# Eight late tiles' second FFN placed between the last scores and the last values; the second stack load three slots earlier

## The chip, the core and the metric

The kernel runs on one core of a Trainium2 chip. The core has five engines that each work through their own instructions in order: PE (TensorE, matrix products), DVE (VectorE), ACT (ScalarE), POOL (GpSimd) and SP (SyncE, which here issues nearly all DMA transfers). They meet only at semaphores. The metric is the device time of one execution in microseconds; a number given for a kernel is the median of several runs. Smaller is better.

## The reference

The input x has 4 batches of 4096 rows of 512 numbers. Three blocks follow each other, each with a residual:

```python
x = x + 0.5 * ffn(layernorm(x), weight, bias)
x = x + attn(layernorm(x), qkv_w, qkv_b, rpb, proj_w, proj_b)
x = x + 0.5 * ffn(layernorm(x), weight, bias)
```

`ffn` is one 512 x 512 product whose two operands are first quantised, in blocks of 32 along the row, to a 6-bit floating-point grid with a scale for each block. `attn` is neighbourhood attention with 16 heads of 32: row i attends to the 13 rows around it (shifted inwards at both ends of a batch), with a relative bias `rpb`:

```python
attn = einsum('bhld,bhlkd->bhlk', q * SCALE, k[:, :, nbr, :]) + rpb[:, bidx]
out  = einsum('bhlk,bhlkd->bhld', softmax(attn), v[:, :, nbr, :])
x_attn = out.reshape(B, L, C) @ proj_w.T + proj_b
```

The two FFNs use the same weights.

## The kernel before

**Tiles and items.** The 16384 rows are 128 tiles of 128 rows (numbered t = 0 to 127). Four tiles make a group of 512 rows; there are 32 groups (8 for each batch). Attention works in items m = 0 to 127: item m is one group and one quarter of the heads (four heads, 128 columns). A product in full precision is split into high and low halves in f16, so each is 12 matmuls of 128 x 512 (function `product`, line 151): low x high, high x low and high x high over four chunks of the inner dimension.

**The order.** The work is put in order by hand. Every stage is a generator; `begin(slot, stage, rank)` enters it at a slot, and each `yield n, rank` moves the rest n slots on. The slots are run one after the other, lower ranks first within a slot, and what a slot emits is appended to the engines' queues in just that order. One step is STEP = 7 slots and handles one tile and one item. The offsets of line 561 place the stages: first FFN of tile t at 7t+5, V product at 7t+20, for item m the query and key projections at 7m+38 (`project_qk`), scores and softmax at 7m+42 (`softmax`), values' products at 7m+59 (`attend`), the output projection of tile t at 7t+93 (`project_out`) and its second FFN 12 slots later (F2 = 12, `second_half`). For the last tiles `out_slot` and `second_slot` give other slots, since the last group's output can only be projected when item 127 has its values.

**A second FFN.** After the output projection of tile t in slot s, `quantised_norms` for the slot s+2 runs over eight slots: POOL forms the factors of the layer norm, ACT applies them, DVE takes the block maxima, POOL scales, ACT rounds to 8 bits, POOL scales back, ACT casts the high half (`hlq`), and in slot s+9 DVE forms the low half and SP issues the transpose `xT<-hlq` (line 205). `second_half(t)` is then 12 matmuls on PE (`pmf<-wt,xT`), in the next slot a multiply-and-add into x on DVE (line 275) and the store of x to the output on SP (line 555). Up to tile 112 the norm of the third block shares its operations with the first norm of tile t+15; from tile 113 on it stands alone.

**The softmax of an item.** Scores on PE in slot a = 7m+42 (144 small matmuls, line 433); then a+1 bias sums on DVE, a+2 maximum on DVE, a+3 subtraction on POOL (467), a+4 exponential on ACT (469), a+5 sums on DVE (472), a+6 scaling on POOL (476), a+8 casts on ACT (480, 481), a+10 the low half on POOL (483) and the transpose `pT<-p` on SP (485). The values' products (line 503, 72 small matmuls) follow in slot a+17, then the copies of their result into `ring` by ACT (530) and DVE (536).

**Values from memory.** The V product is stored to DRAM (line 312), and for each group two "stacks" are loaded back with `load_stack` (line 409), one for each half of the heads, three or six transfers each: the first in slot k+46, the second in slot k+56, with k = 28 x group; rank 9 puts them last in their slot. The second is read by the values of slots k+73 and k+80. There are two buffers (`vsp`), and the one that the second load takes was last read in slot k+52.

**Buffers that matter.** `xp`: 20 buffers of 128 x 512 f32, for the residual tiles x (loaded in slot 7t-18, freed with the store after the second FFN), and for some temporaries of tiles from 123 on. `xtp`: 3 buffers for the transposed xT. `hlp`: 1 buffer for hlq (tiles from 123 on take one of `xp`). `ps_m`: 3 PSUM buffers shared by all 12-matmul products.

The lines that set the late slots:

```python
if i in (-4, -3):                                   # i = t - LAST, LAST = 123
    return (n_items - 1) * STEP + PV + i            # tiles 119, 120: slots 944, 945
if i in (-2, -1):
    return out_slot(NT - 1) + 3 + i                 # tiles 121, 122: slots 960, 961
return out_slot(t) + F2                             # 113 to 118: slots 896, 903, ... 931
```

The last scores stand in slot 931, the values of item 126 in 941, those of item 127 in 948; the output products of tiles 120, 121 and 122 in 929, 933 and 937, those of 123 to 127 in 951 to 959.

Of the kernel before, what the change touches and what calls it, by code (L numbers as in the profile page):

```python
# [26 lines left out]
F32 = mybir.dt.float32  # L27
F16 = mybir.dt.float16
# [9 lines left out]
P = 128  # L38
# [26 lines left out]
def macaron_kernel(  # L65
# [13 lines left out]
    n_batch, length, dim = x.shape  # L79
    xf = x.rearrange("b l c -> (b l) c")  # L80
    of = out.rearrange("b l c -> (b l) c")
    KC = dim // P
# [3 lines left out]
    NT = n_batch * length // P  # L86
# [6 lines left out]
    ps_m = ctx.enter_context(tc.tile_pool(name="ps_m", bufs=3, space=PSUM))  # L93
    ps_s = ctx.enter_context(tc.tile_pool(name="ps_s", bufs=1, space=PSUM))
    ps_v = ctx.enter_context(tc.tile_pool(name="ps_v", bufs=1, space=PSUM))
    xp = ctx.enter_context(tc.tile_pool(name="xp", bufs=20))
    yp = ctx.enter_context(tc.tile_pool(name="yp", bufs=1))
    sm = ctx.enter_context(tc.tile_pool(name="sm", bufs=2))
    q8p = ctx.enter_context(tc.tile_pool(name="q8p", bufs=1))
# [1 line left out]
    xtp = ctx.enter_context(tc.tile_pool(name="xtp", bufs=3))  # L101
# [27 lines left out]
    def bc(t, n):  # L129

        return t.unsqueeze(2).to_broadcast([t.shape[0], t.shape[1], n])
# [30 lines left out]
    def begin(slot, stage, rank=5):  # L162
        slots.setdefault(slot, []).append((rank, stage))
# [19 lines left out]
    def factors(t, which, mv, n=1):  # L183

        rs = sm.tile([P, n], F32, tag=f"rs{which}{n}", name=f"rs{which}_{t}")
        nc.gpsimd.tensor_scalar(  # L186
            rs, mv[:, :n, 1], XS ** -2, LN_EPS * XS ** -2, ALU.mult, ALU.add
        )
        nc.gpsimd.tensor_tensor(rs, rs, minus_half[:, :n], ALU.pow)
        nb = sm.tile([P, n], F32, tag=f"nb{which}{n}", name=f"nb{which}_{t}")  # L190
        if n == 1:
            nc.gpsimd.tensor_scalar(nb, mv[:, 0, 0:1], rs, -1.0, ALU.mult, ALU.mult)  # L192
        else:
            nc.gpsimd.tensor_tensor(nb, mv[:, :n, 0], rs, ALU.mult)
            nc.gpsimd.tensor_scalar(nb, nb, -1.0, None, ALU.mult)
        return rs, nb

    def high(y, hl):

        nc.scalar.copy(hl[:, :, 0, :], y)  # L200

    def low(y, hl, dst):

        nc.vector.tensor_tensor(hl[:, :, 1, :], y, hl[:, :, 0, :], ALU.subtract)  # L204
        nc.sync.dma_start_transpose(out=dst, in_=hl.rearrange("p u s k -> p (u s k)"))
# [14 lines left out]
    def quantised_norms(slot):  # L220

        tiles, mv = together.pop(slot)
        n = len(tiles)
        rs, nb = factors(slot, "q", mv[0], n)
        yield 1, 1

        spare = tiles[0][0] >= NT - GROUP - 1
        if spare:
            y = xp.tile([P, dim], F32, tag="x", name=f"yq{slot}").unsqueeze(1)
        else:  # L230
            y = yp.tile([P, 2, dim], F32, tag="yq", bufs=2, name=f"yq{slot}")[:, :n]
        for u, (t, _) in enumerate(tiles):
            nc.scalar.activation(  # L233
                y[:, u], xs[t], AF.Identity, bias=nb[:, u : u + 1], scale=rs[:, u : u + 1]
            )
        yield 1, 1
        yb = y.rearrange("p u (n q) -> p (u n) q", q=QB)
        sc = sm.tile([P, 2 * NB], F32, tag="sc", bufs=4, name=f"sc{slot}")[:, : n * NB]
        nc.vector.tensor_reduce(sc, yb, AX.X, ALU.max, apply_absolute_value=True)
        nc.vector.scalar_tensor_tensor(  # L240
            sc, sc, F8_SCALE / Q_MAX, least[:, : n * NB], ALU.mult, ALU.max
        )
        r = sm.tile([P, 2 * NB], F32, tag="r", bufs=4, name=f"r{slot}")[:, : n * NB]
        nc.vector.reciprocal(r, sc)  # L244
        yield 1, 1
        nc.gpsimd.tensor_tensor(yb, yb, bc(r, QB), ALU.mult)  # L246
        yield 1, 1
        q8 = q8p.tile([P, 2, dim], F8, tag="q8", name=f"q8_{slot}")[:, :n]
        nc.scalar.activation(q8, y, AF.Identity, bias=nudge, saturate=False)  # L249
        yield 1, 3  # L250
        nc.gpsimd.tensor_tensor(  # L251
            yb, q8.rearrange("p u (n q) -> p (u n) q", q=QB), bc(sc, QB), ALU.mult
        )
        yield 1, 3
        if spare:
            hl = xp.tile([P, dim], F32, tag="x", name=f"hlq{slot}").bitcast(F16)
            hl = hl.rearrange("p (u s k) -> p u s k", u=1, s=2)
        else:
            hl = hlp.tile([P, 2, 2, dim], F16, tag="hlq", name=f"hlq{slot}")[:, :n]
        high(y, hl)  # L260
        yield 1, 1
        xT = xtp.tile([P, 2, 2, KC, P], F16, tag="xT", name=f"xT{slot}")
        low(y, hl, xT[:, :n].rearrange("p u s c q -> p (u s c) q"))
        for u, (t, _) in enumerate(tiles):
            ys[t] = xT[:, u]
# [75 lines left out]
    n_items = n_batch * NG * KC  # L341
# [199 lines left out]
    def project_out(t, slot):  # L541

        r = t * P % RING
        pm = ps_m.tile([P, dim], F32, tag="mm", name=f"pmo_{t}")
        product(
            pm, lambda s, c: ring[:, s, c, r : r + P], lambda s, c: wt[:, s, c, PO : PO + dim]
        )
        yield 1, 8
        nc.vector.scalar_tensor_tensor(xs[t], pm, cp, xs[t], ALU.mult, ALU.add)
        moments(slot, t, "n3")  # L550

    def second_half(t):

        yield from ffn(t, "f2")
        nc.sync.dma_start(out=of[t * P : (t + 1) * P, :], in_=xs.pop(t))
# [3 lines left out]
    STEP = 7  # L559

    F1, V, QK, SC, PV, OUT, F2 = 5, 2 * STEP + 6, 5 * STEP + 3, 6 * STEP, 8 * STEP + 3, 13 * STEP + 2, 12
# [4 lines left out]
    def one(f, *args):  # L566
        f(*args)
        return
        yield

    LAST = NT - GROUP - 1

    def out_slot(t):


        i = t - LAST
        if i >= 0:
            return (n_items - 1) * STEP + PV + 3 + 2 * i
        if i >= 1 - GROUP:
            return LAST * STEP + PV + 21 + 4 * i  # L580
        return t * STEP + OUT

    def second_slot(t):

        i = t - LAST
        if i in (-4, -3):
            return (n_items - 1) * STEP + PV + i
        if i in (-2, -1):
            return out_slot(NT - 1) + 3 + i
        return out_slot(t) + F2  # L590

    for t in range(NT):
        k = t * STEP
        begin(k - 18, one(load, t), 0)
        enlist(k - 10, t, "n1")
        if not 0 < t < EARLY:
            begin(k - 11, one(moments, k - 10, t, "n1"), 1)
        begin(k + F1, first_half(t))
        begin(k + V, values(t))
        begin(k + F1, one(add_bias, t, half_ffn_b), 8)  # L600
        at = out_slot(t)
        begin(at - 5, one(add_bias, t, after_b), 8)
        enlist(at + 2, t, "n3")
        begin(at, project_out(t, at + 2))
        begin(at + 6 if t < LAST else second_slot(t) - 2, one(add_bias, t, half_ffn_b), 8)
        begin(second_slot(t), second_half(t))
    for slot in together:
        if slot >= EARLY * STEP - 10:
            begin(slot, quantised_norms(slot), 1)
    for m in range(n_items):  # L610
        k = m * STEP
# [3 lines left out]
    for n in range(n_batch * NG):  # L615
        k = n * GROUP * STEP
        b, g = divmod(n, NG)
        begin(k + 6 * STEP + 4, one(load_stack, b, g, 0), 9)
        begin(k + 8 * STEP, one(load_stack, b, g, 1), 9)


    with tc.tile_pool(name="setup", bufs=1) as sp, tc.tile_pool(name="scratch", bufs=2) as scr:
# [18 lines left out]
        for _ in quantised_norms(-10):  # L641
            pass
        chunks = (8, 9, 10, 11, 12, 13, 14, 15, 0, 4, 1, 5, 2, 6, 3, 7)
        for o in chunks:
            w, i = (qkv_w, o) if o < 3 * KC else (proj_w, o - 3 * KC)
# [87 lines left out]
        def large(name, o, dt=F32):  # L733
            return scr.tile(
                [P, NB, QB], dt, tag=name, bufs=3 if name == "wu_" else KC, name=f"{name}{o}"
            )

        for o in range(KC):
# [7 lines left out]
            for i, b in enumerate((w_hi, w_lo)):  # L746
                u = large("wu_", f"{o}_{i}")
# [17 lines left out]
        for t in range(1, EARLY):  # L765
            moments(t * STEP - 10, t, "n1")
            for _ in quantised_norms(t * STEP - 10):
                pass
# [94 lines left out]
        slot = first  # L863
# [48 lines left out]
```

## Time and profile before

| | |
|---|---|
| time, median of 3 runs (lowest to highest) | 2408.76 us (2407.12 to 2414.85) |
| the profiled execution: whole time | 2401.24 us |
| its span, first to last instruction | 2399.4 us |
| granted TensorE clock, mean | 0.993 |
| PE busy | 2278.8 us, 95% of the span |
| DVE busy | 2015.3 us, 84% |
| POOL busy | 1989.0 us, 83% |
| ACT busy | 1327.1 us, 55% |
| DMA | 360.58 MB, mean 150 GB/s |

How to read the lines that follow in the text: times are microseconds from the start of the span. In a line of the order of one engine come start, duration, engine, line of the kernel, operation, output<-inputs by name, shape of one instruction and how many were merged (x12). A bracket at the end is the time in which the engine was idle before, and what ended it; "issue" means that the profile shows nothing that it waited for. The page's row of tenths cuts the span in 40 slices of 60 us; 9 means busy for 90% or more. In the chain that ended last each step is followed back to what released it, so its shares say which engine the time hangs on. Matmuls overlap: the time from one product's start to the next one's is what it costs PE.

### The profile page before, as it was taken

How to read it: one execution, taken by the hardware profiler on the slowest of the kernel's cores; microseconds unless marked ns; L12 is line 12 of the kernel's file. 1: busy time of each engine (PE TensorE's matmuls, PEld its weight loads, DVE VectorE, ACT ScalarE, POOL GpSimd, SP SyncE). 2: the span in 40 equal slices, each digit the busy share in tenths (PEclk: the TensorE clock that was granted, in tenths of full speed). 3: DMA queues.
4: the chain of work that ended last, by engine and by line, in shares of the span. 5: the costliest groups of instructions: out<-in, count | busy, mean ns of one | idle time of the engine just before them, and what ended most of it. 6: DMA issues, size and time to landing. Idle time of an engine off the chain costs nothing.

```text
span 2399.4 us, 82333 instructions
## 1 busy us (share of the span) xinstructions
PE 2278.8 (95%) x35539; PEld 1114.0 (46%) x35539; DVE 2015.3 (84%) x3588; ACT 1327.1 (55%) x2080; POOL 1989.0 (83%) x2012
## 2 busy tenths in 40 slices
PE   0799999999999999999999999999999999999987
PEld 0244444444444444444444444444444444444442
DVE  8789888888888888888888888888888888888775
ACT  4455555555555556555555555555555555555442
POOL 5578888888888888888888888888888888888677
PEclk9899999999999999999999999999999999999998
DMA  5788888787787877778867778777778887777753
GB/s 153 145 150 153 158 164 158 148 157 151 145 161 156 152 150 159 146 153 162 161 145 156 150 146 167 153 154 147 159 139 156 158 158 146 162 148 143 137 115 90
DMA packets 925700, 360.58 MB, mean 150 GB/s; under 512 B 718876, under 2 KB 889752, under 8 KB 925336
## 3 DMA queue, kind: packets, MB, share of 16 engines
q1 hardware_dynamic: 924992, 354.79, 75.6%
q8 instruction: 278, 4.55, 0.8%
q10 hardware_dynamic: 344, 0.53, 0.1%
q14 instruction: 86, 0.70, 0.1%
HBM read 110.15 MB, written 67.29 MB: 74 GB/s over the span
## 4 chain that ended last, share of the span: by engine, by line
PE 89%; DVE 4%; DMA 3%; issue 1%; POOL 1%; ACT 1%; SPq 0%; DVEq 0%; ACTq 0%; POOLq 0%
PE pmqk L151 27%; PE pmf L151 26%; PE pmo L151 14%; PE pmv L151 13%; PE ps L433 6%; PE pv L503 3%; DMA xT<-hlq 2%; DVE hlq L204 0%; DVE fw L749 0%; DMA x<-hln 0%; DVE qk L373 0%; DVE stn L180 0%; POOL x L564 0%; ACT ring L530 0%; DVE whl L779 0%
## 5 line engine op out<-in xcount | busy, mean ns | idle before, releaser
L151 PE MATMUL pmf<-wt,xT 128*128 128x512 f16 x3048 | 703.1, 381 | 17.8 <-DMA xT<-hlq 17.7
L151 PE MATMUL pmqk<-x,wt 128*128 128x512 f16 x3072 | 707.7, 380 | 6.2 <-DMA x<-hln 5.4
L151 PEld LDWEIGHTS <-xT 128*128 128x128 f16 x3048 | 297.0, 98 | 386.1 <-DMA xT<-hlq 29.3
L151 PEld LDWEIGHTS <-wt 128*128 128x128 f16 x3072 | 290.0, 98 | 343.1 <-issue 9.7
L151 PE MATMUL pmv<-wt,x 128*128 128x512 f16 x1536 | 353.8, 380 | 5.1 <-DMA x<-hln 5.1
L151 PE MATMUL pmo<-wt,ring 128*128 128x512 f16 x1536 | 355.3, 381 | 2.6 <-issue 2.6
L246 POOL TENSOR_TENSOR yq<-yq,r 128x1024 f32<-128x1024 f32 (+1 forms) x141 | 246.2, 1746 | 130.8 <-DVE r L244 130.8
L564 POOL TENSOR_TENSOR x<-x,half_ffn_b 128x512 f32<-128x512 f32 x256 | 327.4, 1279 | 0.1
L275 DVE SCALAR_TENSOR_TENSOR x<-pmf,coef,x 128x512 f32<-128x512 f32 x256 | 179.5, 701 | 165.2 <-PE pmf L151 164.7
L530 ACT ACTIVATE ring<-pv 128x510 f16<-128x510 f32 (+8 forms) x224 | 82.3, 414 | 400.5 <-PE pv L503 400.5
L310 ACT CAST vt<-pmv 128x512 f16<-128x512 f32 x128 | 74.9, 585 | 389.3 <-PE pmv L151 389.3
L180 DVE BATCH_NORM_STATS2 stn<-x 128x6 f32<-128x512 f32 x384 | 265.3, 691 | 8.9 <-DMA x<-in_L_attn_x_dram 0.2
L251 POOL TENSOR_TENSOR yq<-q,sc 128x1024 f32<-128x1024 fp8e4 (+1 forms) x141 | 246.7, 1749 | 0.4 <-ACT q L249 0.4
L151 PEld LDWEIGHTS <-x 128*128 128x128 f16 x1536 | 150.5, 98 | 187.6 <-DMA x<-hln 5.6
L373 DVE SCALAR_TENSOR_TENSOR qk<-pmqk,qk_b,qk 128x512 f16<-128x512 f32 x256 | 190.6, 744 | 53.8 <-ACT qk L369 53.0
L476 POOL TENSOR_TENSOR sf<-sf,total 128x714 f32<-128x714 f32 (+2 forms) x128 | 178.6, 1395 | 44.2 <-DVE total L474 25.0
L151 PEld LDWEIGHTS <-ring 128*128 128x128 f16 x1536 | 140.2, 98 | 161.5 <-issue 4.2
L186 POOL TENSOR_SCALAR rsq<-mv 128x2 f32<-128x2 f32 (+1 forms) x141 | 131.3, 931 | 96.0 <-DVE mv L181 93.8
L249 ACT ACTIVATE q<-yq,nudge 128x1024 fp8e4<-128x1024 f32 (+1 forms) x141 | 149.9, 1063 | 108.0 <-POOL yq L246 99.8
L369 ACT ACTIVATE qk<-pmqk,qk_b 128x512 f16<-128x512 f32 x256 | 176.1, 688 | 53.2 <-PE pmqk L151 52.1
L233 ACT ACTIVATE yq<-x,nbq,rsq 128x512 f32<-128x512 f32 x254 | 193.0, 804 | 20.8 <-POOL nbq L192 20.2
L467 POOL TENSOR_TENSOR sf<-sf,top 128x714 f32<-128x714 f32 (+2 forms) x128 | 180.4, 1409 | 20.0 <-DVE top L465 19.8
(145 smaller groups left out, 3466.9 us busy)
## 6 DMA issues: line engine op xcount, KB each, us to landing
vs<-vd SPq DMA_DIRECT2D x144, 357.0 KB
x<-in_L_attn_x_dram SPq DMA_DIRECT2D x128, 256.0 KB
vd<-vt SPq DMA_DIRECT2D x128, 256.0 KB
out_dram<-x SPq DMA_DIRECT2D x128, 256.0 KB
vs<-vd SPq DMA_DIRECT2D x24, 378.0 KB
vs<-vd SPq DMA_DIRECT2D x24, 315.0 KB
rows<-in_L_attn_qkv_w_dram SPq DMA_DIRECT2D x12, 256.0 KB
xT<-hlq SPq DMA_TRANSPOSE x141
```

Of the source, the lines that this page charges most:

```text
L151: nc.tensor.matmul(pm, lhs(a, c), rhs(b, c), start=(n == 0), stop=(n == 3 * KC - 1))
L180: nc.vector.bn_stats(st, xs[t])
L233: nc.scalar.activation(y[:, u], xs[t], AF.Identity, bias=nb[:, u : u + 1], scale=rs[:, u : u + 1])
L246: nc.gpsimd.tensor_tensor(yb, yb, bc(r, QB), ALU.mult)
L249: nc.scalar.activation(q8, y, AF.Identity, bias=nudge, saturate=False)
L251: nc.gpsimd.tensor_tensor(yb, q8.rearrange("p u (n q) -> p (u n) q", q=QB), bc(sc, QB), ALU.mult)
L275: nc.vector.scalar_tensor_tensor(xs[t], pm, cf, xs[t], ALU.mult, ALU.add)
L369: nc.scalar.activation(t[:, s, 0, KN:], pms[s], AF.Identity, bias=bias)
L373: nc.vector.scalar_tensor_tensor(t[:, s, 1, KN:], pms[s], bias, t[:, s, 0, KN:], ALU.add, ALU.subtract)
L467: nc.gpsimd.tensor_tensor(s, s, bc(top[:, :n], KN), ALU.subtract)
L476: nc.gpsimd.tensor_tensor(s, s, bc(total[:, :n], KN), ALU.mult)
L564: nc.gpsimd.tensor_tensor(xs[t], xs[t], b, ALU.add)
```

## The change

The second FFN of the eight tiles 113 to 120 (`HELD`) is moved. Those of 113 to 118, which stood at slots 896, 903, 910, 917, 924 and 931, now stand at 932, 935, 938, 942, 943 and 944; those of 119 and 120 move from 944 and 945 to 945 and 946. All eight are now between the last scores (931) and the last values (948). Their DVE sums and stores move with them. Their norms and the transposes into xT stay where they were; since these xT are kept longer, each takes a buffer of `xp` instead of one of the three of `xtp`, and `xp` has 23 buffers instead of 20. Apart from that, in every group the load of the second stack is issued in slot k+53 instead of k+56.

```diff
-    xp = ctx.enter_context(tc.tile_pool(name="xp", bufs=20))
+    xp = ctx.enter_context(tc.tile_pool(name="xp", bufs=23))
...
-        xT = xtp.tile([P, 2, 2, KC, P], F16, tag="xT", name=f"xT{slot}")
+        if tiles[0][0] in HELD and tiles[0][1] == "n3":
+            xT = xp.tile([P, dim], F32, tag="x", name=f"xT{slot}").bitcast(F16)
+            xT = xT.rearrange("p (u s c q) -> p u s c q", u=1, s=2, c=KC)
+        else:
+            xT = xtp.tile([P, 2, 2, KC, P], F16, tag="xT", name=f"xT{slot}")
...
+    HELD = range(NT - 15, NT - 7)
...
-        if i in (-4, -3):
-            return (n_items - 1) * STEP + PV + i
+        if t in HELD:
+            return (n_items - 1) * STEP + PV - (16, 13, 10, 6, 5, 4, 3, 2)[t - HELD[0]]
...
-        begin(k + 8 * STEP, one(load_stack, b, g, 1), 9)
+        begin(k + 7 * STEP + 4, one(load_stack, b, g, 1), 9)
```

## The prediction

> **What bounds the kernel now.** I read the page first (rows of tenths, then the chain that ended last), then the order of PE's instructions over the last 200 us with the idle time in front of each, then all of PE's gaps, then SP's order, then the other engines over the end.
>
> ```profile
> PE   0799999999999999999999999999999999999987
> PE 89%; DVE 4%; DMA 3%; issue 1%; POOL 1%; ACT 1%; SPq 0%; DVEq 0%; ACTq 0%; POOLq 0%
> ```
>
> PE sets the time: it is full from the third slice to the last two and carries 89% of the chain. Between 170 and 2230 us it is busy for 2043.84 of 2060.00 us at a clock of 1.00. After 2330 us it works 47.26 of 69.40 us, at a mean clock of 0.89. So work taken off PE's full stretch and put into the holes of the end is time won. The holes, in PE's order (start, duration, instruction, count, and in brackets the idle time before it with what ended it):
>
> ```profile
> 2324.55 2.75 PE L151 MATMUL pmf<-wt,xT 128*128 128x512 f16 x12
> 2327.23 1.35 PE L433 MATMUL ps<-qk 32*32 32x84 f16 x144
> 2328.51 2.76 PE L151 MATMUL pmo<-wt,ring 128*128 128x512 f16 x12
> 2331.21 0.72 PE L503 MATMUL pv<-pT,vs 126*32 126x30 f16 x72
> 2331.86 2.76 PE L151 MATMUL pmo<-wt,ring 128*128 128x512 f16 x12
> 2341.80 0.83 PE L503 MATMUL pv<-pT,vs 126*32 126x30 f16 x72 [7.18 <-DMA pT<-p]
> 2342.74 7.25 PE L151 MATMUL pmf<-wt,xT 128*128 128x512 f16 x24
> 2355.65 0.76 PE L503 MATMUL pv<-pT,vs 126*32 126x30 f16 x72 [5.66 <-DMA pT<-p]
> 2356.33 15.14 PE L151 MATMUL pmo<-wt,ring 128*128 128x512 f16 x60
> ```
>
> Line 2 is the last scores (item 127); the two L503 lines with brackets are the values of items 126 and 127. Both wait for their transposed probabilities: 7.18 + 5.66 = 12.84 us of idle PE. Between them lie the second FFNs of tiles 119 and 120 (x24); line 1 is that of tile 118.
>
> **Part 1, the held FFNs.** Tiles 113 to 118 leave slots 896 to 931 (PE starts at 2248.84, 2264.90, 2279.91, 2292.49, 2306.79, 2324.55) and go to 932, 935, 938, 942, 943, 944; 119 and 120 move one slot. The same instructions run. A product of 12 takes 2.59 to 2.69 us from start to start.
>
> *What the full stretch gives.* Tile 113: 2.68 us. Tile 114: its scores stand at 2267.59; without its FFN and the 0.90 us that this waits for its xT they can follow the V product at 2263.93: 3.66. Tile 115: 2.68. Tiles 116 and 117 give almost nothing: with no V product left, the FFN is all that stands between the key projection and the scores, which need the low half of the keys. DVE ends that (L373) at 2294.63 and 2308.97, 0.6 and 0.5 us before the scores now start (2295.19, 2309.48). Those scores moreover stop inside for 1.50 and 2.41 us on "issue", until 7.3 and 8.1 us after a stack load began; if the load is what ends these, even that is lost. I take 0 (ends: 0, and 4.7 if the stops vanish too). Tile 118: the output product of tile 120 stands there, so its 2.68 us go, but only for what follows it. Sum ahead of tile 120's product: 2.68 + 3.66 + 2.68 = 9.0.
>
> *What the end can take.* The two waits are ends of a chain with no PE product on it after tile 120's: its sum (DVE L549 at 2325.62), POOL from 2327.31 almost without a break to 2335.5 (L483 of item 126), pT's DMA landing at 2341.7; then for item 127:
>
> ```profile
> 2342.77 0.62 ACT L200 CAST hlq<-yq 128x512 f16<-128x512 f32 x1 [3.30 <-DMA xT<-hlq]
> 2345.81 0.19 POOL L186 TENSOR_SCALAR rsq<-mv 128x1 f32<-128x1 f32 x1 [2.54 <-DVE mv L181]
> 2349.19 1.56 POOL L483 TENSOR_TENSOR p<-sf,p 128x756 f16<-128x756 f32 x1
> ```
>
> The single hlq buffer makes ACT wait for the preceding transpose, DVE's sum and moments of tile 122 queue behind that, POOL's factors behind those, and L483 and pT behind these. This chain moves by the 9.0, no more: values 126 become possible at 2332.7, 127 at 2346.6. PE now has, from the scores at 2315.5: 1.35 scores, FFN 113, product 121, values 125, FFN 114, product 122, FFN 115, that is 5 x 2.6 + 0.7, to 2330.6; a wait of 2.1; values 126; FFNs 116 to 118, to 2341.4. FFN 119 needs a third PSUM buffer back, that of 116, which DVE (slot 943, behind the low half of tile 121 and the ring) frees 0.75 us after its 2351.97, shifted 2343.7: a wait of 2.3. FFN 120 ends at 2348.9, so values 127 come 2.3 us after they could. That is covered: tile 123's product stops for the ring's low half (DVE L536, ended at 2360.06), which queues behind the low half of tile 122 (2357.42 to 2358.6, held by a DMA and not by PE). One more FFN sum (0.7) now lies there; the ring is ready at 2351.8 instead of 2360.06. **The end comes 8.3 us sooner.** Without the cover it would be 2.3 less.
>
> *Other queues.* SP gets a 256 KB store of tiles 113 to 115 ahead of the transposes of items 126 and 127; each waits for a DVE sum that is done 1 us or more before SP reaches the transpose. A store's bytes in front of pT: 0 to 1 us, taken as 0. Buffers: 15 x tiles and 8 held xT make 23 at most, so the pool holds them; three more buffers free no load elsewhere, since a load at slot 7t-18 finds buffers free since slot 7t-34.
>
> *A rule against the row.* The Trainium skill ("TensorE: Matmul & The Clock Gate", HAM oscillation) says that an idle gap over about 3.4 us puts the array on half clock, some 3.4 us of work long. The trace agrees: pmo matmuls last 609 to 634 ns until 2359.5, then 379. By the rule both holes cost 1.7 us more, and filling them brings 12.84 + 3.4 = 16.2. By the rows it is 8.3: the cold FFNs lie inside the wait for pT, the cold products inside the wait for the ring. The remaining waits of 2.1 and 2.3 are below the rule's gap. I go by the rows.
>
> **Part 2, the second stack load.** Same three transfers, from slot k+56 to k+53: on SP it passes one store of V (L312), which waits for DVE, and lands right behind the transposes of slot k+53, exactly where the first stack's load already stands, a step earlier.
>
> ```profile
> 1373.19 1.66 SPq L409 DMA_DIRECT2D vs<-vd  x3
> ...
> 1383.40 2.72 SPq L485 DMA_TRANSPOSE pT<-p  x1
> 1386.44 3.00 SPq L205 DMA_TRANSPOSE xT<-hlq  x1
> ...
> 1396.02 1.67 SPq L409 DMA_DIRECT2D vs<-vd  x3
> ...
> 1401.42 6.32 SPq L485 DMA_TRANSPOSE pT<-p  x1
> 1407.84 3.05 SPq L205 DMA_TRANSPOSE xT<-hlq  x1
> ```
>
> After the first stack SP spends 2.72 us on pT; after the second 6.32, and xT goes out late. PE then waits for xT:
>
> ```profile
> 1413.05 2.76 PE L151 MATMUL pmf<-wt,xT 128*128 128x512 f16 x12 [1.59 <-DMA xT<-hlq]
> 1740.19 1.02 PE L151 MATMUL pmo<-wt,ring 128*128 128x512 f16 x4 [2.13 <-issue]
> ```
>
> Nine such xT gaps stand between 170 and 2270 us, every one 14 to 17 us after a second stack's load and none after a first's: 7.05 us. Less the 0.90 counted above, **6.15 go**. What is late next is pT, used a step later. At the start the second stack of group 0 (142.26) makes PE wait 4.11 us for x2; SP stood idle 1.7 before the V store, so the load can go out at 140.2 and takes 2.06 of it (ends 0 and 4.11). The new place adds a wait for its buffer, read last by the values of slot k+52: PE does those around 1385.3 (one step of 17.6 before 1402.85), SP would get there at 1390.8, so it costs nothing; behind it would queue the V store, the output, the next x and pT.
>
> *The second rule.* The last line above is of another kind: "issue", with nothing to wait for. All fourteen such gaps after 170 us end 7.3 to 13.5 us after a stack load began. The page's q8 queue moves instructions, 4.55 MB in 278 packets, 16 KB each; I take these gaps for code that came late behind the stack's bytes (an inference). The skill ("Runtime: NRT & Kernel Launch", Instruction fetch mechanics) calls crossing a 16 KiB block mostly hidden: by it the move costs 0. By the rows, up to 2230 us seven gaps after first stacks sum to 6.09 and five after second ones to 3.68; in the first one's place the second should cost the first's: **+2.4**. Ends: -3.7 if they vanish, +8.5 for twice the first's. I take the rows.
>
> **The sum.** -8.3 - 6.15 - 2.06 + 2.4 = -14.1 us. The profiled execution, 2399.4 of span and 2401.24 in all, would become 2387.1. It ran below all three timed runs; against their median 2408.76 the same difference gives 2394.7.
>
> **Rivals.** About 0.3% (7.2 us) can be told from no change.
> - *The end does not move* (0.16): the chain to pT grows by what it is given (DVE sums queued before it, stores before pT), and the idle time only changes places. For: it has POOL and one hlq buffer on it; against: POOL has gaps of 2 to 3 us in each step. Part 2 alone: -5.8, so 2403.
> - *All of it* (0.17): the stops inside the scores vanish (4.7 more), the code gaps do not grow (2.4 more) and the start gains fully: about -23, so 2386. For: a PE that waits anyway gives the code time; against: those gaps end by the load, not by PE.
> - *Slower* (0.08): code fetch behind the second load. Six of 30 first loads in the middle stall PE, by 0.81 us each without the tail's and the 1.21 at 251. If every moved load did, 30 x 0.81 = 24 against gains of 16.5: +8, so 2416. It decides from 0.55 us per load on; the first stack, in the same place, shows 0.2.
>
> **Numbers.** Forecast 0.59. Faster: 0.59 + 0.17 = 0.76; same 0.16; slower 0.08. Its own range is 2389 to 2400; to hold 8 in 10 with the unknown costs (code gaps, stores before pT, stops in the scores) it is 2384 to 2407.
>
> **What would show it.** PE's two pT gaps fall from 12.84 to some 2 us, with five FFNs warm at 2.6 us between values 126 and 127; no xT gap follows a second load; SP's pT after it takes under 3 us. Wrong if the way from the first FFN of tile 127 (2243.66) to the last scores, 83.6 us now, shrinks by less than 10, if pT of item 127 lands more than 31 us after the end of its scores (27 now; the scores move by 11.7, the chain by 9.0), or if "issue" gaps after 170 us sum to over 20.

## The result, and the profile after

The changed kernel takes 2394.62 us (median of 6 runs, 2384.24 to 2398.30) against 2410.43 us of the kernel before in the same set (6 runs, 2407.12 to 2418.08). The medians differ by 15.8 us. The ratio on record, formed from all the runs and not from the two medians, is 0.9921, 95% interval 0.9905 to 0.9937: 19 us faster, between 15 and 23. In a second set it was 0.9917 (0.9896 to 0.9938). The forecast was 2394.7 us and 14.1 us of gain (ratio 0.9942): the way and the size are right, and the gain is 2 us (medians) to 5 us (ratio) larger. That the sum came so close is in part luck: two of its terms were off, in opposite ways.

The profiled execution has a span of 2396.5 us, only 2.9 less than the one before (2399.4): it was the slowest of its six runs, and that of before ran below all six of its own. So spans of single executions can't be compared here; stretches can. From the page of the changed kernel, the row of tenths and the chain:

```profile
PE   0799999999999999999999999999999999999998
PE 92%; DVE 4%; issue 1%; DMA 1%; POOL 1%; ACT 1%; SPq 0%; DVEq 0%; POOLq 0%; ACTq 0%
```

The last two slices are fuller (98 where 87 stood), and DMA has fallen from 3% to 1% of the chain. The end in PE's order, from the scores of item 125 on:

```profile
2293.06 2.08 PE L437 MATMUL ps<-qk 32*32 32x84 f16 x144 [2.15 <-DVE qk L377]
2295.07 3.43 PE L151 MATMUL pmo<-wt,ring 128*128 128x512 f16 x12
...
2320.69 1.35 PE L437 MATMUL ps<-qk 32*32 32x84 f16 x144
2321.97 2.76 PE L151 MATMUL pmf<-wt,xT 128*128 128x512 f16 x12
...
2336.34 0.90 PE L507 MATMUL pv<-pT,vs 126*32 126x30 f16 x72 [0.48 <-DMA pT<-p]
2337.17 8.01 PE L151 MATMUL pmf<-wt,xT 128*128 128x512 f16 x36
2347.78 6.95 PE L151 MATMUL pmf<-wt,xT 128*128 128x512 f16 x24 [2.60 <-DVE x L279]
2354.66 0.73 PE L507 MATMUL pv<-pT,vs 126*32 126x30 f16 x72
2355.32 13.20 PE L151 MATMUL pmo<-wt,ring 128*128 128x512 f16 x60
```

The two waits for pT, 12.84 us before, are 0.48 and nothing. In their place stand two other kinds of wait: 2.15 us in front of scores for the low half of the keys (twice; the prediction had named this limit), and 2.60 us in front of FFN 119 for the PSUM buffer of FFN 116 (the prediction had 2.3). And the second stack load in SP's order, one case of 30:

```profile
1394.67 1.66 SPq L413 DMA_DIRECT2D vs<-vd  x3
...
1404.31 2.71 SPq L489 DMA_TRANSPOSE pT<-p  x1
1407.58 2.98 SPq L205 DMA_TRANSPOSE xT<-hlq  x1
```

pT after it takes 2.71 us instead of 6.32. Over the 29 loads of each kind that start between 230 and 2260 us, SP's time for the next pT had a mean of 2.55 us after a first and 5.24 after a second load; now it is 2.59 over both, at most 3.45. The next pT is now issued some 10 us after the begin of a second load, as it was after a first one, and not 5.3. No xT wait is left before the last FFNs.

To compare executions I cut each span in three, at marks that all kernels share: the **start** ends with the projection after the x2 wait near 158 us, the **end** begins with the first FFN of tile 127. "issue" and "xT" are PE's gaps of those kinds in the middle. All in us of one profiled execution:

| kernel | start | middle | end | issue | xT |
|---|---|---|---|---|---|
| before | 162.6 | 2081.1 | 155.8 | 9.8 | 6.2 |
| before_again | 163.1 | 2082.6 | 158.4 | 9.8 | 6.0 |
| held_only | 162.9 | 2082.8 | 144.9 | 10.9 | 5.3 |
| stack_only | 160.0 | 2079.3 | 160.5 | 14.1 | 0 |
| stack_only_again | 155.8 | 2095.3 | 159.2 | 23.1 | 0 |
| stack_only_timed | 159.0 | 2082.7 | 158.1 | 17.2 | 0 |
| after | 163.3 | 2087.6 | 145.6 | 19.2 | 0 |
| both_again | 158.2 | 2083.6 | 145.8 | 16.6 | 0 |
| split | 163.4 | 2065.3 | 145.5 | 4.3 | 0 |
| split_before | 161.6 | 2061.8 | 155.4 | 1.2 | 0 |
| split_six | 161.6 | 2063.4 | 151.8 | 2.4 | 0 |
| split_psum | 158.1 | 2070.7 | 145.9 | 5.8 | 0 |
| split_56 | 157.4 | 2062.3 | 144.3 | 1.1 | 0 |
| six_parts | 157.6 | 2061.7 | 145.7 | 0.5 | 0 |

### The profile page after: what moved, and what is told of

Same layout as the page of the kernel before. It is cut to its first block, busy times and chain, and to the rows that moved or that the text cites. A ratio compares the mean times of both kernels' runs of the same rounds, so it can differ in the third digit from the quotient of the medians.

```text
span 2396.5 us, 82360 instructions
## 1 busy us (share of the span) xinstructions
PE 2285.3 (95%) x35539; PEld 1118.5 (47%) x35539; DVE 2020.8 (84%) x3588; ACT 1329.8 (55%) x2080; POOL 1990.2 (83%) x2012
## 4 chain that ended last, share of the span: by engine, by line
PE 92%; DVE 4%; issue 1%; DMA 1%; POOL 1%; ACT 1%; SPq 0%; DVEq 0%; POOLq 0%; ACTq 0%
PE pmqk L151 28%; PE pmf L151 26%; PE pmo L151 14%; PE pmv L151 14%; PE ps L437 7%; PE pv L507 3%; DVE fw L756 0%; DMA x<-hln 0%; DVE hlq L204 0%; DVE stn L180 0%; DVE whl L786 0%; DMA fw<-in_L_ffn_weight_dram 0%; DVE sc L239 0%; POOL yq L251 0%; DVE x L279 0%
## 5 line engine op out<-in xcount | busy, mean ns | idle before, releaser
L151 PE MATMUL pmo<-wt,ring 128*128 128x512 f16 x1536 | 360.5, 385 | 8.5 <-issue 8.5
L151 PEld LDWEIGHTS <-ring 128*128 128x128 f16 x1536 | 141.6, 99 | 173.2 <-issue 19.9
L487 POOL TENSOR_TENSOR p<-sf,p 128x714 f16<-128x714 f32 (+2 forms) x128 | 192.8, 1506 | 0.1
```

The costliest lines, as they stand in the source:

```text
L151: nc.tensor.matmul(pm, lhs(a, c), rhs(b, c), start=(n == 0), stop=(n == 3 * KC - 1))
L487: nc.gpsimd.tensor_tensor(p[:, :n, KN : 2 * KN], s, ph, ALU.subtract)
```

## The experiments

**The two parts alone.** held_only is the changed kernel with the second load where it was, stack_only the kernel before with that load moved, both_again the changed kernel.

```diff
# held_only
-        begin(k + 7 * STEP + 4, one(load_stack, b, g, 1), 9)
+        begin(k + 8 * STEP, one(load_stack, b, g, 1), 9)
```

> The eight FFNs held back with 23 buffers, the second stack left at slot k+56. Theory: the tail, taken from the start of the first FFN of tile 127 to the end of the span (155.7 us before, 145.6 after), is 145 to 147 us here too, so about 9 to 10 us less time than before; the nine waits for xT after second stack loads stay, some 7 us in the trace. Rival (the change gains by the stack load, the end only moves idle time about): less than 4 us below before.

> Only the second stack load moved from k+56 to k+53. Theory of the prediction: no wait for xT behind second loads (7.05 us before), the tail unchanged at 155 to 156 us, gaps put down to issue a few us larger than the 9.8 of before up to 2230 us, net 3 to 7 us faster. Rival (code fetch takes it all back): the trace shows the xT waits gone but issue gaps of 17 us or more with cold matmuls behind the long ones, and the time is that of before or slower.

> The changed kernel once more, for a second trace of it and a time beside its parts in the same rounds. If the two parts add up, its gain is the sum of those of the two single parts within 3 us. If the first trace's 19.2 us of issue gaps were those of an unlucky execution, this trace shows a sum nearer to 10; if they belong to the load's new place, again 17 to 22, at the same points of the program.

Ratios: held_only 0.9949 (0.9931 to 0.9967), 12.3 us; stack_only 0.9972 (0.9961 to 0.9983), 6.7 us; both 0.9917, 19.9 us. The parts add up (19.0). held_only did what was expected: its end is 144.9 us, and seven xT waits stay. stack_only met both of the opposed expectations in part: the xT waits went and the time fell by about the forecast amount, but the issue gaps rose to 14.1 us, and its end took 160.5 us where 155 to 156 was expected (6.7 us of issue gaps stand there, 3.9 in before). both_again showed the gaps of the middle again (16.6 us), at 11 of the 13 points of the first trace of the changed kernel. So they belong to the load's new place.

**Are gaps and time at odds?** The kernel before and the stack load alone were traced again, and the latter timed again.

> The kernel before, for a second trace of it: if its code gaps are of the same size from execution to execution, they sum to 8 to 12 us up to 2230 us, at most of the same places, and the xT waits to 5 to 8 us; the end from the first FFN of tile 127 is again 155 to 157 us.

> The second stack load alone, for a second trace. If its first trace's 14.1 us of issue gaps up to 2230 us belong to the place k+53, the sum is again 12 to 19 us and mostly at the same points of the program; no xT wait up to 2260 us. If they were chance, the sum is 8 to 12.

> The second stack load alone, timed once more, since its two traces and its first timing (0.9972) disagree. If the first timing holds, the ratio lies between 0.996 and 0.999, and the executions that were traced were slow ones of it. If the traces are typical (issue gaps up by 8 us, xT waits down by 6, start of the kernel 3 us sooner), the ratio is 0.999 to 1.002.

before_again repeats before: 9.8 us of issue gaps, 6.0 of xT; its end, 158.4 us, is a little over the 155 to 157 expected. stack_only_again (one run, 2412.12 us beside a median of 2411.86 of the kernel before) has 23.1 us of issue gaps, above the 12 to 19 expected; the second timing gave 0.9968 (0.9956 to 0.9981), so the first one holds. Over three traces stack_only wins 4.6 us at the start, but its middle is 3.6 us and its end 2.2 us longer than in the traces without the move. That is a gain of nothing in the traces and of 7 us in 44 timed runs. The traced executions are not typical ones: those of before (2401.24 and 2405.84 us) lie 9 and 2 us below the medians of their sets (2410.43 and 2408.02), two of stack_only (2401.60 and 2401.69 us) lie 5 and 2 us above theirs (2396.98 and 2399.79). That is as large as what has to be explained, so these traces can't decide it, and the timing stands. What the issue gaps are in stack_only's faster executions no run here shows; that stays open.

**What the issue gaps are.** They were put down to PE's code. The trace can say more. Counts of matmuls and weight loads from the start of the span to two of the gaps of before (stretch, length, then PE busy with its count and PEld busy with its count):

```profile
0.00:2297.99 2297.99, 2201.95 (x34588) 1079.29 (x34589) 1948.63 (x3464) 1291.03 (x2019) 1915.20 (x1932) 1.00 0.78 153
0.00:2313.15 2313.15, 2214.71 (x34844) 1085.64 (x34845) 1958.83 (x3484) 1298.31 (x2031) 1926.34 (x1943) 1.00 0.78 153
```

34588 + 34589 = 69177 and 34844 + 34845 = 69689: exactly 512 apart. Taken modulo 256, the counts of all gaps of before fall slowly and never rise, 174, 171, 169, 151, ... 64, 57, 57; the slope can be instructions that the trace doesn't count. All other kernels give such a line (174 to 85 where the load is moved). So PE stops only at points that lie a multiple of 256 instructions apart. And the page of before:

```profile
q8 instruction: 278, 4.55, 0.8%
```

2 x 35539 PE instructions / 256 = 277.6 blocks, and the queue that carries instructions moved 278 packets of 16 KB. The times of these packets, which the trace holds too, settle it. In all fourteen traces each of the 137 issue gaps after 170 us ends 1.2 to 1.9 us after a packet of this queue has ended. The packet's place in the queue's order is each time the count before the gap divided by 256 and rounded down: the gap that ends at 2297.99 us (69177 / 256 = 270.2) follows the 270th packet, which ended at 2296.62. So these gaps are PE waiting for its code. In the largest gap of the changed kernel (4.65 us, up to 1973.27) the packet itself took 1.5 us; it had started late, 12.1 us after the one before it, where 7.5 is the median. In the eight traces with whole loads every gap ends 6.4 to 15.3 us after the begin of a stack load. The experiments that follow spread those bytes:

```diff
         for r, s in enumerate((0, 0, 1)):
+            if r:
+                yield 2, 9
             for i, k0, n in runs:
...
-        begin(k + 6 * STEP + 4, one(load_stack, b, g, 0), 9)
-        begin(k + 7 * STEP + 4, one(load_stack, b, g, 1), 9)
+        begin(k + 6 * STEP + 4, load_stack(b, g, 0), 9)
+        begin(k + 7 * STEP + 4, load_stack(b, g, 1), 9)
```

> The changed kernel with the three parts of every stack load issued two slots (5 us) apart instead of back to back. If issue gaps are PE's code blocks queued behind a burst of stack bytes, a part of a third of the bytes holds a block up for less than PE has in hand: the gaps sum to under 5 us and the time is 8 to 15 us below the changed kernel. If they come from the total load on the DMA engines, the gaps stay at 10 to 20 us and the time within 4 us of the changed kernel.

> The kernel before with every stack load's three parts issued two slots apart (first stack in slots k+46, 48, 50, second in k+56, 58, 60), FFNs where they were. If spreading the bytes is what took the 14 us off the changed kernel, the code gaps of the middle fall from 9.8 to under 5 us and the time falls by 8 to 15 us; the two waits for pT at the end stay at 12 to 13 us, and the end from the first FFN of tile 127 stays at 154 to 158 us. Rival (the place behind the transposes, k+53, is needed as well): xT waits stay at 5 us or more and the time falls by less than 6.

split: 2373.69 us, 0.9863 (0.9846 to 0.9879), 14 us below the changed kernel of the same set (2387.99). Its four runs span 4 us, those of the changed kernel 15. split_before, with no FFN held and the second load from k+56: 0.9873 (0.9855 to 0.9892), 30 us, at least twice what was expected, and no xT wait is left either; the two waits for pT stay, 10.7 us in sum where 12 to 13 was expected. So issuing the bytes in one burst was the common cause of both kinds of gap, and the place k+53 isn't needed once they are spread. Spreading also changes what SP issues between the parts; no run separates that from the bytes. Nor is the scatter gone in every kernel with spread loads: five runs of split_psum span 9 us.

The middle falls by 20 us though the gaps that went sum to only 14.7. The two kernels have the same PE instructions in the same order, so their steps can be compared one by one: from before to split_before the steps that hold these gaps shrink by 18.1 us where the idle time in them shrinks by 14.9. A gap is counted from the end of the last matmul, and without one the next matmul would have started before that end, so each gap costs some 0.16 to 0.18 us more than its bracket. A slow clock has no part in it: the granted clock is 1.00 in the middle of both. In the changed kernel it has a part: its middle is 22.3 us longer than that of split, and some 6 us of that are slow matmuls after three of its gaps (3.41, 2.05 and 4.65 us). The last of them, in PE's order:

```profile
1967.80 0.82 PE L151 MATMUL pmo<-wt,ring 128*128 128x512 f16 x3
1973.27 4.02 PE L151 MATMUL pmo<-wt,ring 128*128 128x512 f16 x9 [4.65 <-issue]
```

Nine matmuls take 4.02 us after the gap, where twelve take 2.76; the granted clock is 0.50 from 1973.27 to 1978.0. split_56 goes back to k+56 with held FFNs and spread loads, six_parts halves the parts:

```diff
# split_56
-        begin(k + 7 * STEP + 4, load_stack(b, g, 1), 9)
+        begin(k + 8 * STEP, load_stack(b, g, 1), 9)
# six_parts, from split_56: blocks 0 to 8 and 9 to 17 apart
-            if r:
-                yield 2, 9
+            for lo, hi in ((0, 9), (9, MAXB)):
+                if r or lo:
+                    yield 1, 9
...
```

> The eight FFNs held back, stack loads in three parts two slots apart, the second one from slot k+56 again (56, 58, 60). If held FFNs and spread loads add up, the end from the first FFN of tile 127 is 145 to 146 us and that FFN starts at 2222 to 2226 us, so a span of 2367 to 2372 and a time 2 to 6 us below the split kernel with k+53. If the earlier place is of use once the loads are spread, an xT wait comes back (3 us or more) and the time is above it.

> The same with six parts of half the bytes, one slot (2.5 us) apart, second load from k+56 to k+61. If what counts is how many stack bytes lie in front of a code block at once, the remaining issue gaps (1 to 6 us in the three-part kernels) fall below 1 us and the time is 0 to 4 us lower. If it is the rate at which the bytes arrive (one sixth in 2.5 us is the rate of a third in 5), nothing changes by more than 2 us.

split_56: 2366.39 us, 0.9815 (0.9792 to 0.9838), 45 us faster than before. That is better than expected: the end is 144.3 us (145 to 146 expected), the span 2364.0 (2367 to 2372), no xT wait came back, and the start is 4 to 6 us shorter than in the traces of split_before and split, which no run here explains. six_parts: 2365.91 us, 0.9811 (0.9789 to 0.9834), the same. Issue gaps of 0.5 instead of 1.1 us are all that was left to win, so this run can't tell whether the bytes at once or their rate counts. PE between 170 and 2230 us, before and in split_56 (PE busy comes first after the length):

```profile
170.00:2230.00 2060.00, 2043.84 (x32380) 1004.76 (x32379) 1765.04 (x3102) 1174.65 (x1811) 1766.05 (x1745) 1.00 0.79 153
```

```profile
170.00:2230.00 2060.00, 2058.87 (x32646) 1014.98 (x32631) 1782.67 (x3128) 1183.61 (x1827) 1779.93 (x1761) 1.00 0.78 155
```

16.2 us of idle PE have become 1.1, at nearly the same mean share of the DMA engines (0.79 and 0.78): it was the burst, not the load.

**Two steps of the end,** on the split kernel, whose four runs scattered little. split_psum puts FFN 116 ahead of the values of item 126; split_six leaves FFNs 116 and 117 in their old slots.

```diff
# split_psum
-            return (n_items - 1) * STEP + PV - (16, 13, 10, 6, 5, 4, 3, 2)[t - HELD[0]]
+            return (n_items - 1) * STEP + PV - (16, 13, 10, 9, 5, 4, 3, 2)[t - HELD[0]]
# split_six
-        if t in HELD:
+        if t in HELD and t - HELD[0] not in (3, 4):
```

> The split kernel with the held FFN of tile 116 three slots earlier (939 instead of 942), ahead of the values of item 126, so that DVE can empty its PSUM buffer before the low half of tile 121. If the wait of 2.6 us for a PSUM buffer stands on the path in the end (the ring's low half follows the last values directly in the changed kernel), it goes and the end from the first FFN of tile 127 falls from 145.5 to about 144 or less. If it is covered by the ring as the prediction has it, the end stays within 0.5 us of 145.5.

> The split kernel with the FFNs of tiles 116 and 117 back in their old slots 917 and 924; six are held instead of eight. By the prediction these two give nothing when taken away, since the scores behind them wait for the low half of the keys anyway: the two waits of 2.15 us in front of the scores and the wait for a PSUM buffer go, and the end stays within 1 us of 145.5, or falls by up to 2. Rival (every held FFN saves its 2.6 us): the end grows by 4 to 5 us.

split_psum in PE's order:

```profile
2314.68 2.75 PE L151 MATMUL pmf<-wt,xT 128*128 128x512 f16 x12 [0.69 <-DVE x L279]
...
2328.60 0.73 PE L509 MATMUL pv<-pT,vs 126*32 126x30 f16 x72
...
2333.50 13.22 PE L151 MATMUL pmo<-wt,ring 128*128 128x512 f16 x53 [1.64 <-DVE ring L542]
```

The PSUM wait is 0.69 us instead of 2.59 (split), and the last values start 29.8 us after the last scores instead of 32.3. PE then waits for the ring instead (0.74 and 1.64 us, with slow matmuls behind): the end is 145.9 us against 145.5, the time 2372.81 us (0.9853, 0.9831 to 0.9875). So the wait was covered, in the sense that taking most of it away won nothing. split_six:

```profile
2267.62 4.31 PE L151 MATMUL pmf<-wt,xT 128*128 128x512 f16 x12 [2.60 <-DMA xT<-hlq]
...
2283.77 4.45 PE L151 MATMUL pmf<-wt,xT 128*128 128x512 f16 x12 [1.95 <-DMA xT<-hlq]
```

Its end is 151.8 us, 6.2 longer, and its time 2378.65 us (0.9877, 0.9859 to 0.9896). With tiles 113 to 115 out of the way PE comes to these two FFNs before their xT is there; each waits, and its matmuls then run slowly (granted clock 0.63 and 0.62). The expectation failed and the rival holds for these two, in size even more than it said, though not for its reason.

## The prediction, point by point

- **PE bound, holes at the end: right.** The waits for pT went, and nothing else took their place in full.
- **The end, 8.3 us: right in mechanism, too small.** Mean of before and before_again 157.1, of held_only, after and both_again 145.5: 11.6 us. Within the two first traces it is 10.1: the way from the first FFN of tile 127 to the last scores fell by 13.8 us (83.6 to 69.8) where 11.7 were worked out. The step that was mis-sized is "tiles 116 and 117 give almost nothing ... I take 0": from one output product to the next, their steps fell from 14.29 to 12.83 and from 15.19 to 13.43 us, 3.2 together. The low half of the keys did become the limit, as the line with 2.15 us shows, but the stops of 1.50 and 2.41 us inside those scores were gone (the prediction had this as its upper end, 4.7 us). They stood here in before:

```profile
2295.19 1.30 PE L433 MATMUL ps<-qk 32*32 32x84 f16 x137
2297.99 0.23 PE L433 MATMUL ps<-qk 32*32 32x84 f16 x7 [1.50 <-issue]
2309.48 1.26 PE L433 MATMUL ps<-qk 32*32 32x84 f16 x133
2313.15 0.26 PE L433 MATMUL ps<-qk 32*32 32x42 f16 x11 [2.41 <-issue]
```

  Tile 118 gave 1.7 instead of 2.68, as the product in its step ran at a slow clock. The three tiles ahead gave 8.84 where 9.0 was said. "This chain moves by the 9.0, no more" was too small for the same reason: pT of item 127 is issued 94.9 us after the first FFN of tile 127 instead of 107.1, so it moved by 12.2. And leaving 116 and 117 in place would have cost 6 us, not nothing (split_six).
- **What the end can take: right in the main.** The PSUM wait was 2.60 (2.3 said); the wait for pT of item 126 was 0.48 (2.1 said), since the chain had moved further; the last values stood 34.0 us after the last scores (33.4 said). They came after their pT, and split_psum, where they came sooner, gained nothing. DVE in the changed kernel:

```profile
2352.58 1.10 DVE L204 TENSOR_TENSOR hlq<-yq,hlq 128x512 f16<-128x512 f32 x1 [3.54 <-ACT hlq L200]
2353.60 0.74 DVE L279 SCALAR_TENSOR_TENSOR x<-pmf,coef,x 128x512 f32<-128x512 f32 x1
2354.77 0.75 DVE L279 SCALAR_TENSOR_TENSOR x<-pmf,coef,x 128x512 f32<-128x512 f32 x1 [0.43 <-PE pmf L151]
2356.36 0.84 DVE L540 SCALAR_TENSOR_TENSOR ring<-pv,ring 128x270 f16<-128x270 f32 x3 [0.84 <-ACT ring L534]
```

  The low half of tile 122, the two FFN sums and then the ring's low half: here the ring waits for ACT and so for the values, in split_psum for the queue ahead of it; the ends of the two kernels are within half a microsecond.
- **The clock rule against the row: the row held for the long waits, the rule's limit did not.** The end gained 10.1 to 11.6 us, nearer to the row's 8.3 than to the rule's 16.2. But FFNs 119 and 120 took 6.95 us after a wait of 2.60, "below the rule's gap", at a granted clock of 0.62 in the first 4.4 us.
- **xT waits, 6.15 us: right,** in all five traces with the load moved. Also right: the new place makes SP wait for nothing.
- **The start, 2.06 us: right in the mean, not secured.** 162.9 in the mean of the three traces without the move, 159.3 in that of the five with it; but these five lie between 155.8 and 163.3, and the changed kernel's first trace is the one with 163.3.
- **Code gaps, +2.4 us: right that they grow, too small.** 10.2 us in the mean of three traces, 18.0 in that of five: +7.8, near the upper end of 8.5. The step "in the first one's place the second should cost the first's" failed: the moved loads meet the 256-instruction blocks at other points of the program, and single gaps reached 4.65 us, where 2.13 was the largest in the middle of the first trace. The slow clock after long gaps was not counted (some 6 us in the changed kernel's first trace). The second rule, by which the move costs nothing here, failed by more than the row did. One reading was slightly off: the fourteen gaps end 7.3 to 13.9 us after a load began, not 13.5.
- **Part 2 in sum, -5.8: the timing gives -6.7 and -7.7.** The traces, of executions that were not typical, show no gain; which terms make it up stays open.

## What to carry to other kernels

Before moving a large transfer away from what it disturbs, send it in parts with other work between them: here that removed nearly all of both kinds of gap at once and brought 30 us, where moving it whole brought 7. Idle time with nothing to wait for is worth a count of instructions: gaps at a fixed multiple point to late code, the times of the packets that carry it can confirm it, and an experiment on what they follow tests the cause. When work is taken out of a full stretch, ask what the next instruction waited for anyway, and also what feeds the work that stays.

## What was not expected of the hardware

- PE's matmuls fell to the slow rate after waits much shorter than the 3.4 us of the rule in the prediction (the Trainium skill, "TensorE: Matmul & The Clock Gate", HAM oscillation), and not always: 12 matmuls took 4.45 us after 1.95 (split_six), 2.76 after 1.94 to 1.97 in other places and even after 2.53 (stack_only_again); 24 took 7.0 us after 2.6 in five of the traces and 5.34 in split. The granted clock was 0.84 between 2290 and 2312 us of the changed kernel, where PE waited for 2.15 us twice.
- About 1 MB issued on one queue at once was followed by gaps of up to 4.65 us in which PE waited for its code, and doubled the time that SP spent on a transpose issued 5 us behind it (2.55 to 5.24 us).
